# Pacing the first loads of a per-subject matmul with residual

## The chip, the cores and the metric

The kernel runs on one core of a Trainium2 chip. The metric is the device time of one execution in microseconds (us). Samples are loaded from HBM into SBUF, multiplied, added to themselves and stored back.

## What is computed

Each of 128 samples is a 128 x 1024 matrix in float32. An index per sample chooses one of 8 weight matrices (128 x 128), and the product is added to the sample:

```python
# x: (128, 128, 1024)   subjects: (128,) int32, 0 to 7   weights: (8, 128, 128)
w = weights[subjects]
out = x + jnp.einsum('bct,bcd->bdt', x, w)
```

All of x is read once and all of the output written once: 67.1 MB each way, and 0.5 MB of weights.

## The kernel before

**Tiles.** A group is 4 samples (H = 2 pairs of G = 2), so there are NT = 32 groups and 64 pairs. A sample is 512 KB, a pair 1 MB, a group 2 MB. SBUF has 12 slots (`xs`, SLOTS) for a group each. A sample is loaded into its slot, the sum is written over it in place, and it is stored from there. All weights lie in `w_all`; POOL copies the matrix of each sample into one of four small tiles `ws`. PSUM has two halves (`ps`, P_SLOTS), each of which takes the products of one pair.

**Who does what.** SP issues all loads, one `transfer` (L57) for each sample; the rearrangement in `load` makes four rows of 4 KB into one run of 16 KB in HBM. POOL copies weights (L203). PE makes two matmuls for a sample, 512 columns each (L213). DVE adds a pair at once (L224). ACT issues the stores (L142), which go by group of 2 MB save for the first group and the last, which are stored in smaller pieces. The first pair is also computed by single samples.

**Order.** Everything is issued in an order written out by hand, and each engine runs through its own instructions in order and waits on semaphores. SP first issues sample 0 (x0 below), then `w_all` (L165), then samples 1, 2, 3 and so on (L175). For the first 12 groups nothing in the program holds SP back; from then on it waits (L169 to L172) until the store of the group that had the slot has landed.

**Semaphores.** `s_pair[k][h]` counts the landings of pair h in slot k, 16 for each transfer, and also the stores. `loaded(i, q)` (L117) gives the semaphore and the value that say that the pair of sample q of group i has landed; for sample 0 of group 0 it is the separate `s_first`. POOL's first copy for a pair (L207) waits for it, and PE (L188) does for the first two pairs.

**The end.** SP waits for all stores; ACT issues the last sample's store.

Of the kernel before, what the change touches and what calls it, by code (L numbers as in the profile page):

```python
# [27 lines left out]
G = 2  # L31
H = 2
# [9 lines left out]
DMA = 16  # L42

IDLE = 3

ROWS = 4
QUEUES = {mybir.EngineType.SP: "qSPDynamicHW", mybir.EngineType.Activation: "qActDynamicHW"}
# [2 lines left out]
def transfer(nc, engine, out, in_):  # L50

    later, nc._always_lower_symbolic_ap = nc._always_lower_symbolic_ap, False
    ins, outs = engine.lower_ap_dma(in_), engine.lower_ap_dma(out)
    nc._always_lower_symbolic_ap = later
    return engine.add_instruction(  # L57
        mybir.InstDMACopy(
            name=nc.get_next_instruction_name(),
            engine=engine.engine,  # L60
            ins=ins,
            outs=outs,
            mode="Copy",
            cce_op=ALU.bypass,
            queue=QUEUES[engine.engine],
        )
    )


@with_exitstack  # L70
def kernel(
    ctx: ExitStack,
    tc: tile.TileContext,
    x: bass.AP,
    subjects: bass.AP,
    weights: bass.AP,
    out: bass.AP,
):
    nc = tc.nc
    B, C, T = x.shape  # L80
    S, _, D = weights.shape
    NT = B // (G * H)

    def sbuf(name, *shape, dtype=F32):
        return ctx.enter_context(nc.sbuf_tensor(name, list(shape), dtype)).ap()

    given, near, wrap, index = (
        sbuf(name, 1, B, dtype=I32) for name in ("given", "near", "wrap", "index")
    )
    w_all = sbuf("w_all", C, S, D)  # L90
    ws = [sbuf(f"w{i}", C, 1, D) for i in range(W_SLOTS)]
    zeros = sbuf("zeros", C, N)
    xs = [sbuf(f"x{i}", C, H * G, T) for i in range(SLOTS)]
    ps = [
        ctx.enter_context(nc.psum_tensor(f"ps{i}", [D, G, T], F32)).ap() for i in range(P_SLOTS)
    ]

    s_given = tc.alloc_semaphore("s_given")
    s_wall = tc.alloc_semaphore("s_wall")
    s_index = tc.alloc_semaphore("s_index")  # L100
    s_zeros = tc.alloc_semaphore("s_zeros")
    s_copied = tc.alloc_semaphore("s_copied")
    s_product = tc.alloc_semaphore("s_product")
    s_added = tc.alloc_semaphore("s_added")

    s_pair = [[tc.alloc_semaphore(f"s_pair{i}_{h}") for h in range(H)] for i in range(SLOTS)]


    s_first = tc.alloc_semaphore("s_first")

    def emptied(i, h):


        turns = i // SLOTS
        return (DMA * G + (DMA if h == H - 1 else 0)) * turns

    def loaded(i, q):  # L117

        if i + q == 0:
            return s_first, DMA  # L120
        h = q // G
        return s_pair[i % SLOTS][h], emptied(i, h) + (DMA if i + h == 0 else DMA * G)

    def load(engine, i, q):
        k, h = i % SLOTS, q // G
        transfer(
            nc,
            engine,
            xs[k][:, q, :],
            x[i * H * G + q].rearrange("(a r) t -> a (r t)", r=ROWS),  # L130
        ).then_inc(s_first if i + q == 0 else s_pair[k][h], DMA)

    def store(i, q0, q1):
        k, b = i % SLOTS, i * H * G
        transfer(
            nc,
            nc.scalar,
            out[b + q0 : b + q1].rearrange("g d t -> d g t"),
            xs[k][:, q0:q1, :].rearrange("d (o g) t -> d o (g t)", g=min(G, q1 - q0)),
        ).then_inc(s_first if i + q1 == 1 else s_pair[k][(q1 - 1) // G], DMA)  # L140

    with tc.tile_critical():  # L142

        nc.scalar.dma_start(given, subjects.rearrange("(o b) -> o b", o=1)).then_inc(s_given, DMA)

        nc.vector.memset(zeros, 0.0).then_inc(s_zeros, 1)  # L146
        nc.tensor.wait_ge(s_zeros, 1)
        for _ in range(IDLE):
            nc.tensor.matmul(  # L149
                ps[P_SLOTS - 1][:, G - 1, :N], zeros[:, :D], zeros, start=True, stop=True  # L150
            )

        nc.vector.wait_ge(s_given, DMA)
        nc.vector.tensor_scalar(near, given, -S, S - 1, ALU.max, ALU.min).then_inc(s_index, 1)  # L156
        nc.vector.wait_ge(s_index, 1)
        nc.vector.tensor_scalar(wrap, near, 0, S, ALU.is_lt, ALU.mult).then_inc(s_index, 1)  # L158
        nc.vector.wait_ge(s_index, 2)
        nc.vector.tensor_tensor(index, near, wrap, ALU.add).then_inc(s_index, 1)  # L160
        nc.gpsimd.wait_ge(s_index, 3)


        load(nc.sync, 0, 0)
        nc.sync.dma_start(w_all, weights.rearrange("s c d -> c s d")).then_inc(s_wall, DMA)  # L165
        for i in range(NT):
            k = i % SLOTS
            if i == SLOTS:
                nc.sync.wait_ge(s_first, 2 * DMA)  # L169
                nc.sync.wait_ge(s_pair[0][0], emptied(i, 0))  # L170
            if i >= SLOTS:
                nc.sync.wait_ge(s_pair[k][H - 1], emptied(i, H - 1))  # L172
            for q in range(H * G):
                if i + q:
                    load(nc.sync, i, q)  # L175


        units = [(0, g, g + 1) for g in range(G)]
        units += [(j // H, j % H * G, (j % H + 1) * G) for j in range(1, NT * H)]
        for u, (i, q0, q1) in enumerate(units):  # L180
            k, j = i % SLOTS, i * H + q0 // G
            p = ps[j % P_SLOTS]

            ahead = j < P_SLOTS
            if ahead:
                nc.tensor.wait_ge(*loaded(i, q0))  # L188
            for q in range(q0, q1):
                b = i * H * G + q  # L190
                if b % R == 0:
                    _, subject = nc.values_load_multi_w_load_instructions(
                        index[0:1, b : b + R],
                        engines=[mybir.EngineType.Pool],
                        min_val=0,
                        max_val=S - 1,
                        skip_runtime_bounds_check_because="the index is clamped on the chip above",
                    )
                if b == 0:
                    nc.gpsimd.wait_ge(s_wall, DMA)  # L200
                if not ahead and q == q0:
                    nc.gpsimd.wait_ge(s_added, u - P_SLOTS + 1)
                copy = nc.gpsimd.tensor_copy(  # L203
                    ws[b % W_SLOTS], w_all[:, bass.ds(subject[b % R], 1), :]
                )
                if not ahead and q == q0:
                    copy.wait_op(*loaded(i, q0), "sem-ge")  # L207
            copy.then_inc(s_copied, 1)

            nc.tensor.wait_ge(s_copied, u + 1)  # L210
            for q in range(q0, q1):
                for t in range(0, T, N):
                    mm = nc.tensor.matmul(  # L213
                        p[:, q % G, t : t + N],
                        ws[(i * H * G + q) % W_SLOTS][:, 0, :],
                        xs[k][:, q, t : t + N],
                        start=True,
                        stop=True,
                    )
            mm.then_inc(s_product, 1)  # L220

            mine = xs[k][:, q0:q1, :]
            nc.vector.wait_ge(s_product, u + 1)
            nc.vector.tensor_tensor(  # L224
                mine, p[:, q0 % G : q0 % G + q1 - q0, :], mine, ALU.add
            ).then_inc(s_added, 1)

            if i == 0 or q1 == H * G or i == NT - 1:
                nc.scalar.wait_ge(s_added, u + 1)
                store(i, q0 if i in (0, NT - 1) else 0, q1 - (b == B - 1))  # L230

    with tc.tile_critical() as waits:
        for i in range(NT - SLOTS, NT):
            nc.sync.wait_ge(s_pair[i % SLOTS][H - 1], emptied(i + SLOTS, H - 1))
        nc.sync.wait_ge(s_pair[(NT - 1) % SLOTS][0], emptied(NT - 1 + SLOTS, 0) + DMA)
    last = nc.scalar.dma_start(out[B - 1], xs[(NT - 1) % SLOTS][:, H * G - 1, :])

    tc.add_manual_dep(  # L240
        last.ins,
        waits.name,
        mybir.DependencyInfo(mybir.DependencyClass.NoSync, mybir.DependencyReason.SCHED_ONLY),
        reason="the end of the program waits for it",
    )
# [27 lines left out]
```

## Time and profile before

| What | Value |
|---|---|
| Median of three runs | 326.68 us (326.56 to 326.88) |
| Profiled execution | 326.62 us, of which the span on the core is 324.8 |
| PE busy | 241.5 us (74%) |
| DVE busy | 148.0 us (46%) |
| POOL busy | 34.3 us (11%) |
| Loads: 128 of 512 KB on SP's queue | median 31.9 us from issue to landing |
| Stores of 2 MB: 30 on ACT's queue | median 47.0 us from issue to landing |
| Moved | 134.85 MB, mean 415 GB/s |

The span runs from the first instruction to the last on the core; all times inside the profile count from its start. Engines are PE (matmul), PEld (weight load of the matmul), DVE, ACT, POOL and SP. The DMA row is the mean busy share of the core's 16 DMA engines in each of 40 equal slices, in tenths. A line of a view of stretches gives the stretch, its length, the busy time of PE, PEld, DVE and POOL with the number of instructions, then the granted PE clock, the DMA share and the rate in GB/s. In a line of waits, the engine and its line stand before the arrow, and after it what ended the wait, then the total in us, the number of times and the longest. A landing is the moment at which one of the 16 DMA engines reports its part of a transfer as done; a transfer has 16 of them.

### The profile page before, as it was taken

The numbers are of one execution on the slowest core, as the hardware profiler recorded it, in microseconds if no ns is written. First come the engines' busy times: TensorE is split into PE (matmuls) and PEld (weight loads), VectorE is DVE, ScalarE is ACT, GpSimd is POOL, SyncE is SP. The second block draws the span as 40 slices with busy tenths as digits, with TensorE's granted clock in tenths as the row PEclk, the third lists the DMA queues.
The fourth block names the chain that finished last, engine by engine and source line by source line (L and its number), as shares of the span: only waits on it lengthen the run. The fifth ranks groups of instructions, "written<-read, shape, count | busy, mean of one in ns | idle before, by whom it ended". The sixth has DMA issues, their size and how long they took to land.

```text
span 324.8 us, 1609 instructions
## 1 busy us (share of the span) xinstructions
PE 241.5 (74%) x518; PEld 94.8 (29%) x518; DVE 148.0 (46%) x69; POOL 34.3 (11%) x132
## 2 busy tenths in 40 slices
PE   6999898888888888898888888888899759000000
PEld 2344333333333333333333333333333324000000
DVE  1465555555555555555555554555555552200000
POOL 1011111111111111111111111111101110000000
PEclk9999999999999999999999999999999997855555
DMA  7999999999999999999999999999999999999995
GB/s 244 403 426 420 431 422 420 422 429 431 423 421 432 425 417 425 426 428 428 420 429 424 420 431 422 423 433 425 420 430 416 426 436 417 428 423 431 425 428 235
DMA packets 16218, 134.85 MB, mean 415 GB/s; under 512 B 2641, under 2 KB 3666, under 8 KB 4178
## 3 DMA queue, kind: packets, MB, share of 16 engines
q1 hardware_dynamic: 7184, 67.64, 49.9%
q10 hardware_dynamic: 9026, 67.11, 49.2%
q8 instruction: 4, 0.07, 0.1%
q14 instruction: 4, 0.03, 0.0%
HBM read 67.63 MB, written 67.11 MB: 415 GB/s over the span
## 4 chain that ended last, share of the span: by engine, by line
PE 40%; DVE 21%; issue 17%; POOL 4%; DMA 2%; POOLq 1%; SPq 1%
PE ps L213 40%; DVE x L224 21%; POOL w L203 4%; DMA x<-in_x_dram 2%; POOLq L203 1%; SPq L57 1%; SPq L165 0%; SPq L269 0%; SPq L142 0%
## 5 line engine op out<-in xcount | busy, mean ns | idle before, releaser
L213 PE MATMUL ps<-x,w 128*128 128x512 f32 x512 | 236.9, 608 | 33.6 <-POOL w L203 33.0
L224 DVE TENSOR_TENSOR x<-ps,x 128x2048 f32<-128x2048 f32 (+1 forms) x65 | 146.8, 2259 | 129.3 <-PE ps L213 129.3
L213 PEld LDWEIGHTS ps<-x,w 128*128 128x128 f32 x512 | 93.0, 191 | 177.4 <-issue 94.9
L203 POOL COPY w<-w_all 128x128 f32 x128 | 34.1, 296 | 237.6 <-DMA x<-in_x_dram 219.5
L149 PE MATMUL ps<-zeros 128*128 128x512 f32 x6 | 4.6, 927 | 1.7 <-DVE zeros L146 1.7
L149 PEld LDWEIGHTS ps<-zeros 128*128 128x128 f32 x6 | 1.7, 305 | 3.7 <-issue 2.1
L146 DVE MEMSET zeros<- 128x512 f32 x1 | 0.5, 485 | 1.1 <-SPq L142 1.1
L156 DVE TENSOR_SCALAR near<-given 1x128 int32<-1x128 int32 x1 | 0.2, 215 | 0.6 <-DMA given<-in_itok_B_dram 0.6
L160 DVE CUSTOM_DVE_ANT_0 index<-near,wrap 1x256 uint16<-1x256 uint16 x1 | 0.3, 280 | 0.0
L158 DVE TENSOR_SCALAR wrap<-near 1x128 int32<-1x128 int32 x1 | 0.2, 215 | 0.0
L260 POOL MEMSET const-float32-0.0<- 128x1 f32 x1 | 0.1, 99 | 0.2 <-issue 0.2
L260 POOL MEMSET const-bfloat16-1.0<- 128x1 bf16 x1 | 0.1, 102 | 0.0
L260 POOL MEMSET const-uint8-127<- 128x1 uint8 x1 | 0.1, 102 | 0.0
L260 POOL MEMSET const-float32-1.0<- 128x1 f32 x1 | 0.1, 99 | 0.0
## 6 DMA issues: line engine op xcount, KB each, us to landing
x<-in_x_dram SPq DMA_DIRECT2D x128, 512.0 KB, 31.9
out_dram<-x ACTq DMA_DIRECT2D x30, 2048.0 KB, 47.0
out_dram<-x ACTq DMA_DIRECT2D x4, 512.0 KB, 16.2
out_dram<-x ACTq DMA_DIRECT2D x2, 1024.0 KB, 20.1
w_all<-in_L_cond_weights_dram SPq DMA_DIRECT2D x1, 512.0 KB, 5.0
given<-in_itok_B_dram ACTq DMA_DIRECT2D x1, 0.5 KB
```

The source lines that it names most:

```text
L57: return engine.add_instruction(mybir.InstDMACopy(name=nc.get_next_instruction_name(), engine=engine.engine, ins=ins, outs=outs, mode="Cop ...
L146: nc.vector.memset(zeros, 0.0).then_inc(s_zeros, 1)
L149: nc.tensor.matmul(ps[P_SLOTS - 1][:, G - 1, :N], zeros[:, :D], zeros, start=True, stop=True)
L156: nc.vector.tensor_scalar(near, given, -S, S - 1, ALU.max, ALU.min).then_inc(s_index, 1)
L158: nc.vector.tensor_scalar(wrap, near, 0, S, ALU.is_lt, ALU.mult).then_inc(s_index, 1)
L160: nc.vector.tensor_tensor(index, near, wrap, ALU.add).then_inc(s_index, 1)
L203: copy = nc.gpsimd.tensor_copy(ws[b % W_SLOTS], w_all[:, bass.ds(subject[b % R], 1), :])
L213: mm = nc.tensor.matmul(p[:, q % G, t : t + N], ws[(i * H * G + q) % W_SLOTS][:, 0, :], xs[k][:, q, t : t + N], start=True, stop=True,)
L224: nc.vector.tensor_tensor(mine, p[:, q0 % G : q0 % G + q1 - q0, :], mine, ALU.add).then_inc(s_added, 1)
L260: nc = _bacc.Bacc("TRN2", target_bir_lowering=False, num_devices=1)
```

## The change

While SP issues the loads, it now waits before each of the pairs 2 to 7, counted over all groups. Before pair j + 2 (LEAD = 2) it waits until both samples of pair j have landed, for j from 0 to 5 (PACED - LEAD). `loaded` is called with the second sample of the pair, so for pair 0 the wait is on sample 1. Of samples, at most two pairs (2 MB) are then on their way while this lasts. From pair 8 on the loads go out as before. Nothing else is changed.

```diff
+LEAD = 2
+PACED = 7
...
             if i >= SLOTS:
                 nc.sync.wait_ge(s_pair[k][H - 1], emptied(i, H - 1))
             for q in range(H * G):
+
+                j = i * H + q // G - LEAD
+                if q % G == 0 and 0 <= j <= PACED - LEAD:
+                    nc.sync.wait_ge(*loaded(j // H, j % H * G + 1))
                 if i + q:
                     load(nc.sync, i, q)
```

## The prediction

> **What bounds the kernel.** I read the page's DMA rows first, then the stretches of the run, the waits, SP's timeline, and last the packets and landings of the trace. On the page the 16 DMA engines are busy in every slice but the first and last:
>
> ```profile
> span 324.8 us, 1609 instructions
> PE 241.5 (74%) x518; PEld 94.8 (29%) x518; DVE 148.0 (46%) x69; POOL 34.3 (11%) x132
> DMA  7999999999999999999999999999999999999995
> DMA packets 16218, 134.85 MB, mean 415 GB/s; under 512 B 2641, under 2 KB 3666, under 8 KB 4178
> HBM read 67.63 MB, written 67.11 MB: 415 GB/s over the span
> ```
>
> PE is not the bound: its largest wait, through POOL's weight copies, is for loads (the view of waits):
>
> ```profile
> POOL w L203 <- DMA x<-in_x_dram: 219.5, 58, 6.1
> DVE x L224 <- PE ps L213: 129.3, 65, 6.2
> ```
>
> The stretches show where the transfer rate (last column, GB/s) falls short. This view counts a packet where it starts:
>
> ```profile
> 0.00:8.00 8.00, 5.43 (x8) 2.20 (x9) 1.20 (x4) 1.21 (x8) 1.00 0.77 248
> 8.00:12.00 4.00, 3.53 (x9) 1.40 (x8) 2.35 (x2) 0.00 (x0) 1.00 0.96 397
> 12.00:15.00 3.00, 3.00 (x9) 1.32 (x8) 0.11 (x1) 0.53 (x2) 1.00 0.97 352
> 15.00:20.00 5.00, 5.00 (x14) 2.13 (x13) 3.81 (x2) 0.53 (x2) 1.00 1.02 430
> 40.00:240.00 200.00, 174.53 (x378) 67.86 (x378) 108.46 (x48) 25.60 (x96) 1.00 1.01 425
> 320.00:325.00 5.00, 0.00 (x0) 0.00 (x0) 0.00 (x0) 0.00 (x0) 0.50 0.28 113
> ```
>
> From 15 to 320 us nothing is to be won. I spread each packet over its duration and compare with 427 GB/s, the best steady rate: the loss is 1.44 us from 2.3 us (first packet) to 8, 0.13 from 8 to 12, 0.37 from 12 to 15, some 1.3 from 15 to 318, and the rest at the end, where engines run out one by one. The 16 landings of the last store go from 320.8 to 323.9 us: one engine is 3.1 us behind the first. Each engine has a fixed share of every transfer, so **the end is set by the engine that has lost most time**, not by the mean.
>
> Where engines fall behind, the landings show. w_all's 16 come within 0.44 us (6.13 to 6.57). Those of load x1 (the number is the sample) go from 7.38 to 8.71: twelve engines by 7.82, four at 8.16 to 8.71. Four packets of x1 that start between 5.6 and 5.9 us take 1.6 to 1.9 us, the others some 0.74. These four keep their lateness in x2 to x5. Later, eight packets of instructions (0.3 to 1.1 us each, at 45 us and after) delay single engines too. The change doesn't touch those.
>
> SP's timeline to 8.7 us (start, duration, count) shows what the change bears on:
>
> ```profile
> 0.97 0.56 SPq L57 DMA_DIRECT2D x<-in_x_dram  x1
> 1.58 0.56 SPq L165 DMA_DIRECT2D w_all<-in_L_cond_weights_dram  x1
> 2.19 7.05 SPq L57 DMA_DIRECT2D x<-in_x_dram  x11
> ```
>
> By the landing of x1, SP has issued x0 to x11, one each 0.63 us; at 15.8 us 23 loads are issued and 7 landed, so 16 (8 MB) are on the way. The first store, issued at 10.42, has its first packet at 14.7 and its last landing at 20.0 us.
>
> **What the Trainium skill says**, all on its page "DMA: Bandwidth & Descriptors". "Measured" (under Bandwidth): about 425 GB/s for one core alone; the trace agrees (425). "Queues, rings and completion order": SP and ACT have one ring each on the same 16 engines, which alternate between them by packet; the trace agrees from 15 us on (16 KB load packets of 611 ns between 4 KB store packets of 159 ns), but not for the 4.3 us before the first store packet. "Why a DMA increments its semaphore by 16 and not by 1": only the full 16 says that all has landed, so each new wait is for the slowest engine; the spread of x1 (1.33 us) is an example. "Latency and other measured facts": first byte of a hardware queue after about 0.6 us; here x0 took 1.34 us (0.97 to 2.31), which I use.
>
> **The change part by part.**
>
> 1. Six waits on SP (before pairs 2 to 7, for pairs 0 to 5). SP's semaphore instructions take 0.03 us and stand 0.06 apart in the trace, so 6 x 0.06 = 0.4 us of SP, hidden: SP needs 1.26 us to issue a pair that takes the engines 1.049 MB / 427 GB/s = 2.46 us. Cost 0. Behind the waiting SP stand only later loads; w_all is already issued. POOL's copies, and PE behind them, wait for these loads.
>
> 2. Issues moved. x0 to x3 and w_all keep their times, to 4.0 us. x4 moves from 4.19 to the landing of x1, 8.71 + 0.05; its packets come 1.34 later, at 10.1. The engines end x3 between 9.6 and 10.9 (landings 9.99 to 11.27, less 0.4, the distance from the last load packet's end to its landing). So the four late engines have x4 in time, and twelve run dry for 0.2 to 0.5 us. A first packet after idleness took some 1.06 us against 0.62 (x0's 16), so 0.4 more: up to 0.9 us for these. They are over 1 us ahead of the four, so I put it at 0, with +0.9 as the bound, should one of them be the last at the end. The next round is x3 landing at 11.27, x6's packets at 12.7, engines out of x5 from 12.6: no gap worth counting. In a steady round, 0.4 + 0.05 + 1.34 = 1.8 us lies within the 2.46 us of the pair still on the way, leaving 0.66.
>
> 3. Stores start earlier. At 10.42 only x3's rest, x4 and x5 are ahead of the first store, not a dozen loads: some 2.5 us of work, so I expect its first packet near 13 rather than 14.7. The slow read-only stretch (12 to 15; read packets of 0.65 to 0.85 us instead of 0.61) would shrink. Bounds: 0 (the slowdown belongs to the switch to stores) and -0.37 (all of it). I take -0.37, as store traffic gave the full rate within a microsecond of starting.
>
> 4. SP issues nothing between 4.0 and 8.7 us. Before, four loads went out in 4.2 to 6.7, as the four packets stalled. If filling the rings caused that, the four win 1.05 us and nothing runs dry in part 2. How much reaches the end? The last landings are 323.89, 323.26, 322.68: with the last engine alone among the four, 0.63; all of 1.05 if the next is too; none if neither. The trace doesn't name engines. Bounds 0 and -1.05; I take -0.5.
>
> 5. After pair 5 (about 24 us; before, x11 landed at 23.75) SP has pairs 6 and 7 on the way instead of a dozen loads, and issues 0.83 MB a microsecond, twice what the engines move: nothing runs dry. Bytes, compute and the store-only tail from 271 us on are the same. Cost 0.
>
> Sum: 0 + 0 - 0.37 - 0.5 + 0 = -0.87 us. The profiled execution took 326.62 (span 324.8 and 1.8 around it), so 325.75; the median is 0.06 above it: **325.8 us**, a gain of 0.27%. Some 0.2% (0.65 us) is about what a measurement here can tell from no change.
>
> **Rivals.**
>
> *Transfers hidden anyway.* The stalls come from w_all's 1024 small packets just before, not from the queue; the slow reads are the price of switching to stores. For it: all packets at 14.0 to 14.5, just before the first store, are slow (0.85). Against: reads were already slower from 12.5. Then at most half of part 3 remains: -0.2, **326.5 us**.
>
> *Engines run dry.* The place is the wait before x4. The price is the dry gap and restart of part 2, 0.9 us less at most 0.2 of part 3: +0.7, **327.4 us**. It decides if an engine of the twelve ends last, which two instruction packets of 1.0 to 1.1 us on one engine suffice for. For it: four late engines hold back the twelve others, whose work can't be shared out again. Against: these twelve have over 1 us of slack at that point. If the loop of 1.8 us were above 2.46, all engines would run dry in each round before the stores; x0's first landing (4.34 - 0.97, less its 1.23 of transfer) makes it 2.2 at the worst.
>
> That the waits don't bite is excluded: SP is eight loads ahead at the first of them.
>
> **How the numbers follow.** Forecast 0.44, hidden 0.31, dry 0.25. The forecast's own range is 325.2 to 326.0: parts 3 and 4 in full give -1.42. With the rivals, 324.9 to 327.5: the lower end leaves 0.3 for a luckier order of late engines, the upper reaches the dry case.
>
> **What would show it.** Right: x4 issued near 8.8 us, or 7.9 if the four packets are quick; x1's landings within 0.6 us; first store packet near 13 us; over 400 GB/s in 12 to 15; last landings less than 3.1 us apart. Hidden: x1 still spread by 1.3 us, the end the same. Dry: packets starting at 10.1 that take over 1 us, a dip from 9.6 to 10.5, no smaller spread at the end. It is wrong altogether if the rate after 25 us is other than 425.

## The result

The changed kernel takes 329.19 us (median of 10 runs, 327.84 to 331.08) against 326.84 us before (10 runs, 326.49 to 327.80): ratio 1.0072, 95% interval 1.0054 to 1.0090. It is 2.35 us slower, where 0.87 us of gain was forecast, and outside the range. The profiled execution took 330.08 us, 0.9 above the median; its span is 3.5 us longer than before.

### The profile after

The lines of the page that answer to those of before:

```profile
span 328.3 us, 1609 instructions
PE 241.7 (74%) x518; PEld 94.5 (29%) x518; DVE 148.0 (45%) x69; POOL 34.3 (10%) x132
GB/s 242 318 421 402 419 417 426 426 427 421 425 427 424 426 425 420 423 426 427 425 424 424 420 423 432 422 421 430 426 424 423 425 425 420 427 425 426 427 427 185
HBM read 67.63 MB, written 67.11 MB: 410 GB/s over the span
```

Work and bytes are the same. The rate is lower in the second slice (8 to 16 us; 318, and 403 before) and in the fourth (25 to 33 us), and then as before, to the last slice. The stretches, from the changed kernel:

```profile
8.00:12.00 4.00, 3.70 (x10) 1.44 (x9) 2.45 (x2) 0.00 (x0) 1.00 0.90 315
12.00:15.00 3.00, 2.66 (x7) 0.87 (x5) 0.30 (x1) 0.00 (x0) 1.00 0.95 285
15.00:20.00 5.00, 3.70 (x8) 1.44 (x8) 2.02 (x2) 0.69 (x3) 1.00 0.99 399
20.00:40.00 20.00, 16.07 (x34) 6.54 (x35) 11.43 (x5) 2.52 (x10) 0.97 0.98 409
40.00:240.00 200.00, 175.72 (x381) 68.93 (x380) 107.72 (x47) 25.08 (x94) 0.99 1.01 425
```

In 12 to 15 us the DMA share (last column but one) is 0.95 while the rate is 285 GB/s: the engines are occupied with packets that progress slowly. Such a share is not a rate.

The waits of SP show the new wait at its full count, and its timeline (three windows) when the released pairs went out:

```profile
SPq L61 <- DMA x<-in_x_dram: 17.9, 6, 4.3
```

```profile
8.41 1.11 SPq L61 DMA_DIRECT2D x<-in_x_dram  x2
10.93 1.81 SPq L61 DMA_DIRECT2D x<-in_x_dram  x2
15.61 1.13 SPq L61 DMA_DIRECT2D x<-in_x_dram  x2
```

I measure the loss as in the prediction: packets spread over their durations, compared with 427 GB/s. "Idle" is the part in which fewer than 16 packets are under way; the rest is packets that take longer than at that rate.

| Stretch (us) | Loss before (idle) | Loss after (idle) | More |
|---|---|---|---|
| 2.3 to 8 | 1.44 (0.14) | 1.45 (0.77) | 0.0 |
| 8 to 15 | 0.51 (0.01) | 1.89 (0.61) | 1.38 |
| 15 to 40 | 0.08 (0.00) | 1.12 (0.44) | 1.04 |
| 40 to 318 | 1.23 (0.27) | 1.24 (0.27) | 0.0 |

So 2.4 us are lost between 8 and 40 us, and never won back: the last store's 16 landings are 2.44 us later on average. They go from 322.97 to 327.35 us, 4.4 us apart (3.1 before), which is some 1 us more for the engine that ends last. The sum is the 3.5 us between the two profiles.

Inside the first stretch: x1 lands from 7.28 to 8.40, x4 is issued at 8.41 and has its first packet at 9.8. From 9.5 to 10.5 us only 12 of 16 engines have a packet; then, until 14.5 us, the packets of 16 KB that start in each half microsecond take 0.8 to 1.4 us on average instead of 0.62. Not all are slow: their median is 0.75 us, and a tenth take over 1.6. x6, issued at 10.93, has its first packet near 14.3.

### The profile page after: what moved, and what is told of

It is laid out like the page before. It is cut to its first block, busy times and chain, and to the rows that moved or that the text cites. A ratio compares the mean times of both kernels' runs of the same rounds, so it can differ in the third digit from the quotient of the medians.

```text
span 328.3 us, 1609 instructions
## 1 busy us (share of the span) xinstructions
PE 241.7 (74%) x518; PEld 94.5 (29%) x518; DVE 148.0 (45%) x69; POOL 34.3 (10%) x132
## 4 chain that ended last, share of the span: by engine, by line
PE 38%; DVE 22%; issue 18%; POOL 4%; DMA 2%; POOLq 1%; SPq 1%
PE ps L221 38%; DVE x L232 22%; POOL w L211 4%; DMA x<-in_x_dram 2%; POOLq L211 1%; SPq L61 1%; POOLq L200 1%; SPq L169 0%; POOLq L146 0%; SPq L277 0%; SPq L146 0%
```

## Experiments

Theories, as named in the expectations. **L**: a load released so late leaves the read rings (SP's queue on the 16 engines) dry, and that costs the time. **S**: stores that start early disturb the reads. **W**: the waits cost in themselves. Later **Q**: a short queue in itself makes reads slow. **D**: the first store's coming makes reads slow. Each ratio is to the kernel before, run on the same chip; its median was 326.8 to 326.9 us.

### Three pairs on the way

```diff
-LEAD = 2
-PACED = 7
+LEAD = 3
+PACED = 8
```

> LEAD = 3, PACED = 8: six waits as in the changed kernel, but three pairs on their way. Theory L (the read rings run dry because 3 to 4 us pass from a landing to the first packet of the load that it releases, more than the 2.46 us of the one pair left): two pairs left are 4.9 us, so the reads stay fed and the time is 326.8 to 327.3. Theory S (stores that start early disturb the reads): the first store still finds six loads at most before it, at least 328. Theory W (the waits cost in themselves): 329, as in the changed kernel.

326.90 us, ratio 0.9999 (0.9991 to 1.0008). Six waits that do bite (11.7 us in all; x6 goes out at 8.15 us instead of 5.46) cost nothing once a third pair is on the way. Its stretches are those of a fed ring:

```profile
8.00:10.00 2.00, 2.00 (x6) 0.95 (x5) 0.89 (x1) 0.00 (x0) 1.00 0.98 410
10.00:12.00 2.00, 2.00 (x5) 0.68 (x4) 1.51 (x2) 0.00 (x0) 1.00 1.01 418
12.00:15.00 3.00, 3.00 (x8) 1.33 (x7) 0.58 (x2) 0.53 (x2) 1.00 1.00 386
```

The loss from 8 to 15 us is 0.32, 0.19 less than before, and the time doesn't show it. W falls.

### Eight pairs on the way

```diff
-LEAD = 2
-PACED = 7
+LEAD = 8
+PACED = 13
```

> LEAD = 8, PACED = 13: the same six waits, before pairs 8 to 13 for pairs 0 to 5, with eight pairs on their way, about what was on the way without any wait. Theories L and S: no difference from before, 326.5 to 327.1. Theory W: 328 to 329.

326.87 us, ratio 1.0001 (0.9993 to 1.0009). Three of these six waits hold SP (3.7 us in all). Together with the six waits of the kernel with three pairs, W is out.

### One wait

```diff
-PACED = 7
+PACED = 2
```

> PACED = 2: only the wait before pair 2 for pair 0 is left; all later loads go out as before. Theory L: the gap at 9.5 to 12 us alone, 0.7 to 1.1 us lost, 327.5 to 328. Theory S: the queue is short when the first store comes at 10.2 us, so the whole loss, 328.5 to 329.5. Theory W: one wait of six, 327.2.

328.77 us, ratio 1.0053 (1.0040 to 1.0066). One wait of six makes most of the loss, if not all: its interval overlaps that of the changed kernel. This is more than L said and within reach of S's number; but the first store decides against S: here its first packet comes at 15.4 us, later than before (14.7), and the reads are slow all the same:

```profile
8.00:10.00 2.00, 2.00 (x6) 0.93 (x5) 0.84 (x1) 0.00 (x0) 1.00 0.81 336
10.00:12.00 2.00, 1.77 (x4) 0.50 (x4) 1.51 (x2) 0.00 (x0) 1.00 1.05 336
12.00:15.00 3.00, 2.77 (x7) 0.95 (x5) 0.30 (x2) 0.00 (x0) 1.00 0.84 229
15.00:20.00 5.00, 4.18 (x10) 2.00 (x11) 2.54 (x2) 1.06 (x4) 1.00 1.00 416
```

The lowest rate is at 12 to 15 us, 3.5 us and more after SP issued x4, although x4 to x11 have gone out by 13.8. The loss from 8 to 15 is 2.09 (0.71 idle), 1.58 more than before; from 15 to 40 it is 0.20.

### The four later waits

```diff
-                if q % G == 0 and 0 <= j <= PACED - LEAD:
+                if q % G == 0 and 2 <= j <= PACED - LEAD:
```

> Only the waits before pairs 4 to 7 (for pairs 2 to 5); x0 to x7 go out freely. Theory L: nothing lost up to 14 us; then what the trace of the changed kernel shows after 15 us beyond that of before (0.37 from 15 to 20, 0.50 from 20 to 30, 0.17 from 30 to 40), so about 327.9. Theory S: the first store finds a longer queue, starts near 14.5 us as before, and the time is 326.8 to 327.2. Theory W: four waits of six, 328.4.

327.19 us, ratio 1.0008 (1.0000 to 1.0016), much less than L's 327.9. The loads do come to a stop here: x8 is issued at 13.65 and its first packet is at 17.3, when x7 has landed at 16.98. But x0's and x1's stores are under way, and the rate holds:

```profile
12.00:15.00 3.00, 3.00 (x8) 1.33 (x7) 0.23 (x2) 0.53 (x2) 1.00 0.96 348
15.00:20.00 5.00, 5.00 (x13) 2.26 (x12) 3.86 (x2) 0.53 (x2) 1.00 1.03 429
```

Here a stretch without load packets cost nothing, as stores covered it.

### When x4 goes out

Four kernels have one wait before pair 2, but for other events. All later loads are free.

```diff
-PACED = 7
+PACED = 2
...
-                    nc.sync.wait_ge(*loaded(j // H, j % H * G + 1))
+                    nc.sync.wait_ge(s_wall, DMA)    # early_release
+                    nc.sync.wait_ge(s_copied, 1)    # release_7
+                    nc.sync.wait_ge(s_copied, 3)    # release_8
```

The events are the landing of the weights, POOL's first copy, and its copies for pair 1. release_11 waits at the same place for pair 1 to land, written with LEAD = 1:

```diff
-LEAD = 2
-PACED = 7
+LEAD = 1
+PACED = 1
...
-                if q % G == 0 and 0 <= j <= PACED - LEAD:
+                if q % G == 0 and j == 1:
```

> One wait before pair 2 as in the kernel with one wait, but for the landing of the weights (6.4 us) instead of pair 0 (8.4 us): x4 goes out 2 us earlier, with x1 to x3 (1.5 MB) still on the way, and all later loads follow freely. Theory L (late release leaves the read rings dry): x4's packets are there by 7.9 us, engines end x3 from 9.6 us, so 326.6 to 327.1. Theory Q (it is the short queue in itself, not the gap, that slows the reads until it has filled again): still over 327.7.

> One wait before pair 2, all later loads free, as with one wait; the wait is for POOL's first weight copy, so x4 goes out near 7.1 us, 2.5 us before the first engine needs it at 9.6. If 1.34 us from issue to first packet were what a release needs (the prediction's value): no loss, 326.6 to 327.2. Theory L with a lead of about 3 us needed (6.5 was free, 8.5 cost 2 us): 327.2 to 327.8.

> The same with the wait for POOL's copies for pair 1, so x4 goes out near 7.8 us, 1.8 us before it is needed. With 1.34 us: still no loss, 326.6 to 327.2. Theory L with about 3 us: 327.8 to 328.4.

> The same with the wait for pair 1 (x3) instead of pair 0, so x4 goes out near 11.0 us, 1.4 us after it is needed, with nothing but the first store (10.3 us) for the engines. Theory L with about 3 us: 4.4 us of the lead are lacking, less up to 1.2 us in which the store of x0 fills them, 329.5 to 331. With 1.34 us: 2.7 less 1.2, 328 to 328.8. The first store finds empty rings: if what it waits for is the loads ahead of it, its first packet comes under 2 us after its issue (4.3 in the kernel before); if 4 us are its own latency, near 14.4.

| Kernel | x4 issued (us) | Median (us) | Ratio (95%) | Loss 8 to 15 (idle) |
|---|---|---|---|---|
| before | 4.19 | 326.8 to 326.9 | 1 | 0.51 (0.01) |
| early_release | 6.54 | 327.09 | 1.0009 (1.0001 to 1.0017) | 0.34 (0.03) |
| release_7 | 6.92 | 326.73 | 0.9999 (0.9991 to 1.0006) | 0.52 (0.02) |
| release_8 | 7.96 | 327.24 | 1.0006 (0.9998 to 1.0014) | 1.36 (0.44) |
| one wait | 8.53 | 328.77 | 1.0053 (1.0040 to 1.0066) | 2.09 (0.71) |
| release_11 | 11.00 | 329.54 | 1.0069 (1.0055 to 1.0083) | 2.95 (2.09) |

Each loss is that of one profiled execution. Up to 6.92 us there is nothing that grows with the delay (at most 0.3 us in a median). With a fresh release and the rings as short as 1.5 MB the reads keep their rate, so Q falls at that length:

```profile
10.00:12.00 2.00, 1.95 (x5) 0.68 (x4) 1.48 (x2) 0.00 (x0) 1.00 0.94 385
12.00:15.00 3.00, 3.00 (x8) 1.33 (x7) 0.49 (x1) 0.54 (x2) 1.00 1.02 380
```

My figure of 3 us for the lead falls too: 2.7 us (6.92, needed at 9.6) is enough. Between 6.92 and 8.53 us the loss sets in. At 7.96 us (release_8, a lead of 1.6 us) the median shows hardly any, while the trace loses 0.85 us more than before. From there 0.57 us later in the issue add 1.5 us to the median. The next 2.5 us, up to release_11, add only 0.8: one store of 0.5 MB fills 1.2 us of that gap.

The trace of release_8 also shows where L is too simple:

```profile
10.00:12.00 2.00, 2.00 (x6) 0.87 (x5) 1.51 (x2) 0.00 (x0) 1.00 1.04 262
12.00:15.00 3.00, 2.48 (x6) 0.76 (x4) 0.79 (x2) 0.06 (x1) 1.00 0.83 339
```

The packets of x4 follow those of x3 and hardly an engine is idle up to 11.0 us, yet two packets that start at 10.1 us take 1.9 and 2.6 us. From 11.0 to 12.5 us three to six of the 16 engines have no packet, although x5 to x8 were issued from 8.47 to 10.39 us and no engine has done its part of x5 (first landing at 13.67). With one wait it is the same: at 13.0 to 13.5 us five engines are idle, while x6, issued at 9.69, first lands at 15.34. So a late release is followed by some microseconds in which loads that are issued come slowly or not at all. That an empty ring brings this about is argued, not shown. With 1 MB left, as in release_8, the short queue itself is not excluded.

release_11 also answers for the store. Its stretch from 10 to 12 us is empty:

```profile
10.00:12.00 2.00, 1.86 (x6) 0.55 (x5) 1.51 (x2) 0.00 (x0) 1.00 0.19 76
12.00:15.00 3.00, 2.72 (x7) 0.94 (x5) 0.39 (x2) 0.00 (x0) 1.00 0.98 299
```

The first store, issued at 10.46, has its first packet at 11.66: 1.2 us into empty rings, 4.3 behind loads in the kernel before. And x4, issued at 11.00 right behind that store, waits 2.3 us, until the store's packets are through (13.1). Here what was issued first was served first. That is no rule: in the kernel before, the first store overtook more than half of the dozen loads ahead of it.

### Half a pair more

```diff
-                if q % G == 0 and 0 <= j <= PACED - LEAD:
+                if q % G == 1 and 0 <= j <= PACED - LEAD:
```

> The six waits stand before the second sample of each pair instead of the first: 2.5 MB on the way at most and 1.5 MB at the release (3.7 us of transfer). Theory L: 3.7 us about cover the 3 to 4 us from landing to first packet, so between three pairs and two, 326.9 to 327.5. Theory Q: near the changed kernel, 328 or more.

327.42 us, ratio 1.0016 (1.0009 to 1.0023), as L said. No engine is idle from 8 to 15 us (0.02), yet 0.97 us are lost, 0.46 more than before: from 10 to 14 us packets take 0.80 us on average, most of them 0.61 to 0.65 and single ones up to 2.4. Here and in release_8 slow packets come before any gap. (The profiled execution is the slowest of the 21.)

### First stores held back

ACT holds the first two stores until pair 1 is added; once on the order of before, once with the one wait.

```diff
-PACED = 7
+PACED = 1    # held_stores; 2 with the one wait
...
-                nc.scalar.wait_ge(s_added, u + 1)
+                nc.scalar.wait_ge(s_added, max(u + 1, 3))
```

> The kernel before, but ACT holds the stores of x0 and x1 until pair 1 is added (about 17.3 us instead of 10.4 and 12.1). Theory D (the slow reads at 12 to 15 us come from the first store's coming): 12 to 15 us run at over 410 GB/s and the slow packets move to about 19 to 22 us. If they belong to the loads: 12 to 15 us stay at 350 to 395 GB/s. Time 326.3 to 327.1 either way, 0.37 us being at stake.

> The kernel with one wait, with the stores of x0 and x1 held until pair 1 is added. Theory D: the loss from 12 to 15 us (1.25 in the kernel with one wait) falls to under 0.5 and the time to 327.6 to 328.1, the gap at 9.5 to 12 us remaining. If the slow reads are a consequence of the gap alone: 12 to 15 us lose over 1 us as before, and 328.5 to 329.

Without a wait on SP (PACED = 1 leaves none): 327.21 us, ratio 1.0010 (1.0004 to 1.0017), just above the 327.1 expected. The trough at 12 to 15 us is gone (352 before), as D said:

```profile
12.00:15.00 3.00, 3.00 (x8) 1.33 (x7) 0.10 (x1) 0.53 (x2) 1.00 1.03 421
15.00:20.00 5.00, 5.00 (x13) 2.24 (x12) 3.86 (x2) 0.53 (x2) 1.00 1.00 406
```

But reads alone then run on at 0.64 us a packet (0.61 beside stores), and what is saved from 8 to 15 us (0.28) is lost from 15 to 40 (0.33). That trough held nothing to win.

With the wait: 328.37 us, ratio 1.0052 (1.0036 to 1.0069), between the two ranges expected. From 12 to 15 us it loses 0.75 instead of 1.25, so D may have a part there (one execution each); but 8 to 15 together still lose 1.79, without a store near:

```profile
10.00:12.00 2.00, 1.84 (x6) 0.54 (x5) 1.51 (x2) 0.00 (x0) 1.00 0.92 311
12.00:15.00 3.00, 2.73 (x7) 0.95 (x5) 0.37 (x2) 0.00 (x0) 1.00 0.96 322
```

So the slow packets after the gap (0.65 to 0.99 us on average in each half microsecond from 11 to 14 us) need no store.

## Why the prediction was wrong

The rival "engines run dry" came true: its place (the wait before x4), its sign, and its first gap. It had 0.25, and its price was too small: +0.7 us, 2.35 measured.

**Part 1, the waits: right.** Cost 0 (three pairs on the way, ratio 0.9999; eight, 1.0001).

**Part 2, the moved issues: this step failed.** It put at 0 what measured 1.38 us. Its times were right: x4 issued at the landing of x1, first packet 1.39 us later (1.34 predicted), a part of the engines dry. Three things were not.
- I put the gap at 0, as the twelve engines had slack against the four late ones. But the loss is not confined to the gap: 8 to 15 us lose 1.38 more than before as a mean over all engines, of which 0.60 is idle and 0.78 slow packets. I had allowed one slow packet for each engine (0.4 us); they went on for 4 us, and engines stood idle beside loads that were issued (4.6 of 16 at 12.0 to 12.5 us, with x5 issued at 8.93 and done on none).
- "No gap worth counting" in the next round took 1.34 us again. x6, issued 0.7 us after the first store, took 3.4. The 4.3 us between the first store's issue and its first packet, in the trace of before, had shown that an issue waits behind the other queue; I applied it to stores only. Nor is a store needed for such a delay: with one wait, loads issued at 9.69 or before left engines idle at 13.0 us, ahead of any store.
- The bound of +0.9 rested on the same two errors.

**Part 3, earlier stores: right on the time, wrong on the worth.** First packet at 12.8 us (13 predicted), gain 0 instead of 0.37; the held stores show why.

**Part 4, the four late packets of x1: wrong.** SP issued nothing between 4.0 and 8.4 us, and x1 still landed in two lots, eight engines by 7.63 and eight from 7.97 to 8.40. So the spread does not need the filling of the rings. The -0.5 had no support but coincidence in time.

**Part 5, after pair 5: wrong in size.** 15 to 40 us cost 1.04 more, not 0. With reads behind, POOL and PE come late (PE starts pair 2 at 16.2 us instead of 14.5), and stores with them. At 23 and at 31 us hardly a load packet is under way, and stores cover it (x14: issued at 28.37, first packet at 32.36, behind a 2 MB store). From 26.5 to 28.5 us neither ring has enough, and two to four engines are idle: no more than 2 MB of loads are on the way, and the store issued at 26.49 hardly moves before 29. The later waits alone don't do this (1.0008); that it takes the first ones as well is argued from this.

In sum, parts 2 and 5 cost 1.38 and 1.04 us where both stood at 0, and parts 3 and 4 gave nothing of their 0.87. That makes 2.4 us, close to the 2.35 between the medians.

The end: the last engine is 4.4 us behind the first instead of 3.1. Which delays add up there is not shown, as packets don't name their engine. Nor is it shown why loads come slowly for some 4 us after a late release; the experiments exclude only a store as the main cause, and a short queue for a single release with 1.5 MB left.

No version beat the kernel before: three pairs, the early releases and the held stores are at best equal.

## What to carry to other kernels

Where transfers bound a kernel, a cap on what is on its way must leave more work in the rings than passes between a landing and the first packet of the load that it releases; here 1 MB left (2.46 us on average, but 1.1 us for the engine that was furthest ahead) was too little, and 2 MB were free. Leave room: a lead of 1.6 us still lost 0.85 us in its trace, and 2.7 us lost nothing. Don't price that delay from the first transfer of the run alone: it was 1.3 us there, 1.4 for x4, and 3.4 for x6 two loads later. And in these runs a gap cost more than its length and was not won back, save where stores filled it.

## Not expected of the hardware

- After a late release the slowest tenth of the 16 KB packets from 10 to 14 us took over 1.2 to 1.8 us (single ones up to 2.6), while the median was 0.62 to 0.76 (0.61 to 0.64 in a fed ring): the changed kernel, one wait (with and without the stores), release_8 and half a pair. In the last two they came before any gap. Where a gap came, the loss from 8 to 15 us was 1.4 to 3 times the idle time (release_11: 2.09 idle, 2.95 lost; one wait: 0.71 and 2.09).
- In that time engines stood idle beside issued loads: six of 16 in release_8 at 11.5 to 12.0 us, with four loads issued and not done.
- The first store took 1.2 us from issue to first packet on empty rings, 2.5 with two loads ahead, 4.3 with a dozen; a load behind stores took 2.3 to 4.0 us. The wait did not grow with the whole of the queue: with a dozen loads ahead, the store overtook more than half of them.
- Reads alone took 0.64 us a packet from 13 to 20 us (held stores), and 0.61 when mixed with stores.
